# A windowed-attention layer and a per-image depthwise convolution: another order for the first rounds

## The chip, the core and the metric

The kernel runs on one core of one Trainium2 chip. Its metric is the device time of the whole launch in microseconds. A core has five engines with a queue of instructions each: PE (TensorE, the matrix unit), DVE (VectorE), ACT (ScalarE), POOL (GpSimd) and SP (SyncE, which here issues transfers only). They meet through semaphores.

## The reference, cut to what matters

The input is x, 16 images of 192 channels and 56 x 56 pixels, float32. The first layer is one shifted-window attention block, the second a depthwise convolution whose taps are computed from each image:

```
h   = window(roll(norm(x; g1, b1), -3))             # windows of 7x7 = 49 tokens
q,k,v = (h @ qkv_w + qkv_b)                         # 6 heads of 32
a   = softmax(q*scale @ k.T + bias[rel] + mask)     # mask: -inf in windows cut by the shift
x1  = x + unroll(a @ v @ proj_w + proj_b)
y   = x1 + gelu(norm(x1; g2, b2) @ fc1_w + fc1_b) @ fc2_w + fc2_b
t   = relu(batchnorm(mean(y) @ w1.T));  wt = t @ w2.T + b2    # taps of each image
out = depthwise3x3(y, wt * causal mask) + bias
```

All the products are in float32.

## The kernel before, in words

**Tiling.** The 192 channels are 3 groups (G) of 64; the 128 partitions hold 64 channels of two different window rows. An image has 8 window rows, so 4 steps of two window rows each (NU = 4); the launch has S = 64 steps. A step's tokens are 392 (UT) on each half.

**Rounds.** The loop `for r in range(-2, S + 3)` (L1620) is a software pipeline. In a steady round r it runs the scores and values of step r, the weighted sum, projection and residual of step r-1, the first feed-forward layer of step r-2 and the second of step r-3, the queries and keys of step r+1 and the first norm's statistics of step r+2. Rounds -2 to 2 are shorter: they have no feed-forward layers yet, but they load the parameters and fold the norms' gains and shifts into the weights.

**Who does what in a step.** `statistics` (L292) squares on ACT and adds the three groups on POOL into `fold`. In the early rounds `full_deviations` (L381) turns them, with a product against the constant block `full` (four recorded products, L387), into the reciprocal deviations `rb[:, 0]` on all partitions: PE, then ACT (L395), DVE (L402), ACT (L409, L413). Later rounds use `deviations` (L312), which computes a few rows only (L322) and spreads them through a buffer in memory, `rsd`, with three transfers on SP (L369, L378). `scaled1` (L424, mostly POOL, L436 and L447) multiplies x by `rb` into `xs`; `scaled2` (L459, POOL) does so for the second norm. `queries_keys` (L470) makes three products: part 0 is read by ACT into q (L491), part 1 by DVE into kbd (L502), and part 2 (heads 4 and 5) by ACT and DVE in turns into q2 and kbd2 (L515, L525, L534). `scores` (L544) makes three products j = 0, 1, 2 (L558) and for each a chain: add the bias table (DVE L584), maximum (DVE L595), subtract (POOL L600), exp (ACT L607), sum and reciprocal (DVE L612, L613), multiply (POOL L618). `values` (L653) makes three products (L673) that ACT copies (L689), and sends them in eight transfers on SP (L699). `turn_shares` (L622) turns the shares on DVE (L629) and sends them in ten transfers on SP (L635); `turn_values` (L704) turns the values (DVE L708). `weighted` (L711) makes the weighted sums (L728), copied out of PSUM by ACT (L755) and, for j = 1, by DVE (L757). `projection` (L773; L799, L785) is added to x by DVE (L827). `first_layer` (L831, L838) and `second_layer` (L856, L876) follow.

**PSUM.** Four tiles of two banks go round in the order in which the program takes them (`bank`, L187), so a product may wait for the reader of the tile four takings earlier.

**Parameters.** `load_qkv` (L1280) brings the attention weights raw, in five column blocks and two copies, ten transfers, half on SP and half on ACT. `small_loads` (L1203) puts eleven small vectors on ACT's queue; `small_columns` (L1236) transposes them on PE. `fold_qkv` (L1396) and `fold_fc1` (L1454) take the channel means off the weights: `centred_weights` (L1354) with wide products (L1362) and DVE (L1378), `shift_products` (L1333) with products of one column (L1342); `fold_qkv_rest` (L1415) and `fold_v` (L1427, L1435) do the rest for heads 4 and 5 and for the values. `biases_of_positions` (L1470) builds the bias tables `bt1` and `bt2` from transfers through memory (L1493, L1507), the masks (L1481) and twelve sums on DVE (L1522); half of them (r = 1) serve only an image's last step.

**The order.** Every operation is given to `Plan.add` (L53) with its engine, an assumed duration, what it reads and writes, and for transfers an assumed time to land (`lag`) or a fixed due time (`by`). `Plan.order` (L72) keeps PE's operations in the order of the program, derives due times for the others from that, and on each other engine always takes the operation that can start first, and among those the one due first. So PE's order is written by hand in the loop, and the others' follows from the assumed durations.

```
late[i] = ideal[i] if op[0] == "PE" else ideal[i] + op[5]
...
key=lambda j: (max(ready[j] - free[e], 0.0), late[j], j),
```

## Time and profile before

| | |
|---|---|
| three runs | 2743.76, 2746.55 and 2738.92 us, median 2743.76 us |
| the profiled execution | 2747.47 us, of which the span from first to last instruction is 2745.6 us |
| mean granted clock of PE | 0.995 |
| busy share | PE 98%, DVE 72%, ACT 62%, POOL 57% |
| PE from 0 to 150 us | 123.17 us busy, granted clock 0.92 |
| PE from 150 to 400 us | 249.83 us busy, granted clock 1.00 |
| PE from 2690 us to the end | 45.04 of 55.6 us busy |
| start of the first feed-forward product (L838) | 119.69 us |

In the views, "PE" is a product and "PEld" a load of weights for it; "SPq" and "ACTq" are transfers being issued. A row of the view by stretches gives the stretch and its length, the busy time and count of PE, PEld, DVE, ACT and POOL, the granted clock of PE, the busy share of the transfer engines and their rate. A row of the timeline gives start, length, engine, line and operation, the count, and in brackets the idle time before it with what ended it. The profile records one product of the program as two instructions; counts here are those of the records.

### The profile page before, as it was taken

The page shows a single profiled execution, that of the slowest core. Times are in us where ns is not written, and L with a number is a line of the kernel's source. Part 1 is how long each engine was busy: PE and PEld are TensorE (multiplying, and loading weights), DVE is VectorE, ACT ScalarE, POOL GpSimd, SP SyncE. Part 2 cuts the span into 40 slices and gives each one's busy share as a digit, 9 for nine tenths or more (in the row PEclk, how much of TensorE's full clock was granted, in tenths as well). Part 3 has the DMA queues.
Part 4 walks back from the last instruction along what each step waited for, and adds up shares of the span by engine and source line. Part 5 has one row for each costly group of instructions (what it writes and reads, how often), then busy time and mean ns, then how long its engine had stood idle before and what let it go on. Part 6 is the DMA issues. An engine that isn't in the chain of part 4 may idle for free.

```text
span 2745.6 us, 78133 instructions
## 1 busy us (share of the span) xinstructions
PE 2703.0 (98%) x32871; PEld 1669.1 (61%) x32871; DVE 1966.0 (72%) x3462; ACT 1714.7 (62%) x2787; POOL 1552.0 (57%) x1433
## 2 busy tenths in 40 slices
PE   6999999999999999999999999999999999999998
PEld 4656666666666566566566566566566566666654
DVE  6765776767687676876768777676876767767674
ACT  4556667657567566666666666576666666676553
POOL 6565565565565565565665555555655655655532
PEclk9899999999999999999999999999999999999999
DMA  5623343334425334343343424344253343433231
GB/s 124 127 51 72 83 111 71 86 83 104 92 67 117 69 86 101 72 116 72 78 104 90 106 67 96 73 103 92 67 129 69 75 110 80 113 72 73 60 77 52
DMA packets 142563, 239.61 MB, mean 87 GB/s; under 512 B 35148, under 2 KB 100612, under 8 KB 142212
## 3 DMA queue, kind: packets, MB, share of 16 engines
q1 hardware_dynamic: 140360, 232.95, 37.9%
q8 instruction: 258, 4.23, 0.7%
q10 hardware_dynamic: 1852, 1.66, 0.3%
q14 instruction: 93, 0.76, 0.1%
HBM read 66.81 MB, written 38.98 MB: 39 GB/s over the span
## 4 chain that ended last, share of the span: by engine, by line
PE 96%; DVE 2%; SPq 1%; DMA 0%; issue 0%; ACT 0%; POOL 0%; ACTq 0%; DVEq 0%
PE ps L876 28%; PE ps L838 28%; PE ps L478 14%; PE ps L673 7%; PE ps L558 5%; PE ps L799 5%; PE ps L728 5%; PE ps L785 2%; PE ps L322 2%; DVE sq L972 0%; PE ps L1362 0%; DVE hid L1152 0%; DMA tt<-in_L_conv_qkv_w_dram 0%; PE ps L1342 0%; DVE bt L1522 0%
## 5 line engine op out<-in xcount | busy, mean ns | idle before, releaser
L876 PE MATMUL ps<-hid,wf 128*64 128x392 f32 x4608 | 774.3, 494 | 0.5 <-issue 0.5
L838 PE MATMUL ps<-xs,wf 64*128 64x392 f32 x4608 | 769.5, 489 | 0.0
L838 PEld LDWEIGHTS ps<-xs,wf 64*128 64x128 f32 x4608 | 445.9, 187 | 312.6 <-issue 0.9
L876 PEld LDWEIGHTS ps<-hid,wf 128*64 128x64 f32 x4608 | 330.0, 137 | 408.2 <-issue 369.8
L306 POOL TENSOR_TENSOR fold<-sq 128x392 f32<-128x392 f32 x127 | 129.6, 1021 | 692.9 <-PE ps L322 684.3
L618 POOL TENSOR_TENSOR e<-e,tot 128x784 f32<-128x784 f32 x192 | 321.4, 1685 | 212.2 <-DVE tot L613 208.6
L850 ACT ACTIVATE hid<-ps,b1f 128x784 f32<-128x784 f32 x384 | 342.0, 913 | 137.3 <-PE ps L838 135.0
L478 PE MATMUL ps<-xs,wqkv 64*128 64x392 f32 x2304 | 402.6, 499 | 3.5 <-DVE x L827 1.5
L1152 DVE SCALAR_TENSOR_TENSOR y<-x,wt,y 128x770 f32<-128x770 f32 x270 | 319.1, 1201 | 66.2 <-ACT y L1014 45.3
L478 PEld LDWEIGHTS ps<-xs,wqkv 64*128 64x128 f32 x2304 | 218.6, 188 | 164.9 <-issue 17.0
L600 POOL TENSOR_TENSOR e<-e,top 128x784 f32<-128x784 f32 x192 | 283.3, 1504 | 41.6 <-DVE top L595 41.6
L491 ACT ACTIVATE q<-ps,qbs 128x400 f32<-128x400 f32 (+1 forms) x128 | 68.5, 589 | 319.6 <-PE ps L478 319.6
L612 DVE TENSOR_REDUCE tot<-e 128x16 f32<-128x784 f32 x192 | 182.2, 949 | 107.6 <-ACT e L607 107.6
L755 ACT COPY o<-ps 32x392 f32<-32x392 f32 x512 | 244.3, 477 | 9.5 <-PE ps L728 3.2
L629 DVE STREAM_TRANSPOSE tt<-e 128x512 f32<-128x512 f32 x384 | 245.7, 684 | 1.9 <-POOL e L618 0.4
L766 ACT ACTIVATE x<-x,vecs 128x392 f32<-128x392 f32 x192 | 105.7, 613 | 208.2 <-POOL xs L447 203.5
L343 DVE TENSOR_TENSOR m<-ps,m 128x196 f32<-128x196 f32 (+1 forms) x64 | 23.2, 363 | 273.5 <-ACT m L336 273.5
L673 PE MATMUL ps<-xs,wqkv 64*64 64x196 f32 x4608 | 204.7, 327 | 3.4 <-issue 1.4
L463 POOL TENSOR_TENSOR xs<-x,rb 128x392 f32<-128x392 f32 x192 | 193.5, 1039 | 25.0 <-DMA rb<-rsd 25.0
L306 POOL TENSOR_TENSOR fold<-x 128x392 f32<-128x392 f32 x128 | 132.8, 1038 | 127.7 <-DVE x L827 99.8
L436 POOL TENSOR_TENSOR xs<-x,rb 128x343 f32<-128x343 f32 x191 | 186.0, 1003 | 22.2 <-DMA rb<-rsd 16.8
L584 DVE TENSOR_TENSOR e<-ps,bt 128x784 f32<-128x784 f32 x192 | 175.3, 968 | 12.5 <-ACT hid L850 7.4
(134 smaller groups left out, 3688.1 us busy)
## 6 DMA issues: line engine op xcount, KB each, us to landing
pt<-tt SPq DMA_DIRECT2D x256, 192.0 KB
vb<-kbd SPq DMA_DIRECT2D x488, 96.0 KB
x<-in_x_dram SPq DMA_DIRECT2D x112, 294.0 KB
out_dram<-y SPq DMA_DIRECT2D x135, 196.0 KB
pt<-tt SPq DMA_DIRECT2D x256, 96.0 KB
rb<-rsd SPq DMA_DIRECT2D x118, 196.0 KB
out_dram<-y SPq DMA_DIRECT2D x45, 154.0 KB
x<-in_x_dram SPq DMA_DIRECT2D x16, 168.0 KB
```

Source lines behind the costliest of these rows:

```text
L306: at.tensor_tensor(f, src[:, 0], src[:, 1], ALU.add)
L463: nc.gpsimd.tensor_tensor(xs2[:, g], xv[:, g], rb[:, 1], ALU.mult)
L478: nc.tensor.matmul(p[:, ab, 0:UT], lhs_qk(ab, g, i), d[P(ab), g, 0:UT], start=(g == 0), stop=(g == G - 1), tile_position=(64 * ab, 0),)
L600: nc.gpsimd.tensor_tensor(ev, ev, top[j].broadcast_to([128, 16, N]), ALU.subtract)
L618: nc.gpsimd.tensor_tensor(ev, ev, tot[j].broadcast_to([128, 16, N]), ALU.mult)
L629: nc.vector.transpose(tt[:, kb, 16 * j : 16 * j + 16], src)
L673: nc.tensor.matmul(p[P(wh), ab, 0 : 4 * N], wqkv[P(ab), g, 2 * DIM + 64 * m : 2 * DIM + 64 * m + 64], xs[P(ab), g, wh * 4 * N : (wh + 1) * ...
L755: add("ACT", 0.5, lambda dst=dst, src=src: nc.scalar.copy(dst, src), [k], [("o", j, i)])
L838: nc.tensor.matmul(p[:, ab, 0:UT], wf1[P(ab), g, f * 128 : (f + 1) * 128], xs2[P(ab), g], start=(g == 0), stop=(g == G - 1), tile_position ...
L850: nc.scalar.activation(hid[:, f], p[:, :, 0:UT], AF.Gelu, bias=b1f[:, f : f + 1])
L876: nc.tensor.matmul(p[P(ab), 0, 0:UT], wf2[:, f, g * 64 : (g + 1) * 64], hid[:, f, ab], start=(f == 0), stop=(f == NFC - 1), tile_position= ...
L1152: nc.vector.scalar_tensor_tensor(dst, s_, w[:, g, t : t + 1], dst, ALU.mult, ALU.add)
```

## The change

- **Unread products.** A new helper `warm` issues n products with `full` as weights into the PSUM tile that is next in turn, which nobody reads: eleven of 128 columns at the very start, two of 392 after the first x has come, two after its square, two after the first `rb`, two after the first `xs`.
- **Weights in two transfers.** `load_qkv` brings the whole matrix once on SP and once on ACT. The columns then lie in the order of the input, so `centred_weights` writes four blocks with their own keys, and part 2 takes its columns from two places.
- **Transfers elsewhere.** The masks go to ACT's queue; the transfers of the bias rows get due times ahead of the load of step 1, which itself is due earlier.
- **Bias tables in two parts** with a key each, (bt, 0) and (bt, 1); only an image's last step reads the second. Their assumed duration is larger.
- **Another order of PE.** In round 0 what is still to fold, part 2 of the queries and `fold_v` move from round -1 to between the scores j = 1 and j = 2. In round 1 the first value product of step 1 stands before the scores j = 2. `weighted(0)` moves ahead of the value products of step 2. In round 2 `scaled1(3)` and the queries of step 3 come before `fold_fc1`, and the first norm of step 4 moves behind the projection.
- **fc1's fold.** Its wide products and its products of one column alternate instead of following each other.
- **Step 0's second norm** takes `full_deviations(1)` instead of `deviations([1])`, so without the transfers through memory. `deviations([1])` stays in round 3.
- **Copies.** For steps 0 and 1 the copies of j = 1 go from DVE to ACT. The assumed time to land of the shares is 2.5 instead of 7 us for steps 0 to 2.

The diff, cut to its core:

```
+    def warm(n, src, keys):
+        i = taken[0] % 4
+        def go():
+            for _ in range(n):
+                nc.tensor.matmul(ps[i][:, 0, 0 : src.shape[1]], full, src, start=True, stop=True)
+        add("PE", n * 0.00167 * src.shape[1], go, keys + ["blk"], [("ps", i, 0), ("ps", i, 1)])
...
-    def full_deviations():
+    def full_deviations(n=0):
...
-    def scores(s):
+    def scores(s, amid=None):
...
+            if j == 2 and amid is not None:
+                amid()
...
-            add("DVE", 0.98, biased, [pk, "bt"] + ["variance"] * (j == 0), [("e", j)])
+            add("DVE", 0.98, biased, [pk, ("bt", 0), ("bt", int(last))] + ["variance"] * (j == 0), [("e", j)])
...
-                lag=7.0,
+                lag=7.0 if s > 2 else 2.5,
...
-        yield
+            yield
...
-                if j != 1:
+                if j != 1 or s < 2:
...
+        dup(
+            lambda p: wraw[p],
+            wv,
+            [("wqkvl",)],
+            queues=("SP", "ACT"),
+            dur=0.8,
+            by=-99.5,
+            lag=7.0,
+        )
...
         def means():
-            for i, at, pieces_ in parts:
-                lo, hi = pieces_[0][0], pieces_[-1][1]
+            shifts = shift_steps(n, chunks, p)
+            for i, lo, hi, _ in parts:
                 for g in range(G):
                     nc.tensor.matmul(
...
+                    next(shifts, None)
...
-            add("SP", 0.72, go, [], [("relrows", yq)], lag=4.0, by=-79.0)
+            add("SP", 0.72, go, [], [("relrows", yq)], lag=3.5, by=-98.0)
...
-                    add("DVE", 0.2 + 0.1 * (hi - lo), go, keys, ["bt"])
+                    add("DVE", 0.1 + 0.32 * (hi - lo), go, keys, [("bt", r)])
...
+    def last_heads():
+        fold_qkv_rest()
+        queries_keys(0, (2,))
+        fold_v()
...
-            load(1, -80.0, 5.0)
+            load(1, -97.0, 5.0)
+            warm(11, full, [])
+            statistics(0, 0)
+            warm(2, rows(0)[:, 0].rearrange("p r c -> p (r c)"), X(0))
+            warm(2, sq[:, 0], ["sq"])
             small_columns(0)
-            statistics(0, 0)
...
+        if has(r) and r != 2:
+            ahead = values(r)
+            scores(r, {0: last_heads, 1: lambda: next(ahead)}.get(r))
+            for _ in ahead:
+                pass
+        if r == 2:
             scores(r)
+            scaled1(3)
+            queries_keys(3, (0, 1, 2))
             fold_fc1()
+            full_deviations(1)
+            scaled2(0)
+            weighted(1)
+        if r == 3:
             deviations([1])
...
+            if r == -1:
+                warm(2, rb[:, 0], RB(0))
             scaled1(r + 1)
-        if early and r > -2:
+        if -2 < r < 2:
             if r == -1:
+                warm(2, xs1[:, 0], [("xs1", 0)])
                 queries_keys(0, (0, 1))
-                fold_qkv_rest()
-                queries_keys(0, (2,))
-                fold_v()
...
+        if has(r - 1) and r != 2:
+            weighted(r - 1)
         if r == 1:
             ahead = values(2)
-            next(ahead)
+            for _ in range(G):
+                next(ahead)
             fold_taps()
-        if has(r - 1):
-            weighted(r - 1)
...
+        if r == 2:
+            full_deviations()
```

## The prediction

> **What bounds the kernel now.** First the page's parts 1 and 2: PE is the bound, and only the first slice shows room.
>
> ```profile
> span 2745.6 us, 78133 instructions
> ...
> PE 2703.0 (98%) x32871; PEld 1669.1 (61%) x32871; DVE 1966.0 (72%) x3462; ACT 1714.7 (62%) x2787; POOL 1552.0 (57%) x1433
> ```
>
> Next the view by stretches (PE's busy time is the third column; after POOL's comes the granted clock):
>
> ```profile
> 0.00:10.00 10.00, 0.00 (x0) 0.00 (x0) 4.16 (x15) 0.00 (x0) 9.15 (x18) 1.00 0.66 129
> 30.00:40.00 10.00, 4.85 (x117) 3.61 (x120) 9.14 (x15) 4.38 (x8) 4.45 (x4) 0.97 0.66 169
> 70.00:80.00 10.00, 7.03 (x118) 5.18 (x120) 7.64 (x14) 7.75 (x17) 7.12 (x6) 0.85 0.44 96
> 80.00:90.00 10.00, 9.72 (x175) 7.58 (x171) 7.73 (x19) 5.46 (x11) 3.67 (x6) 0.64 1.00 204
> 110.00:120.00 10.00, 7.81 (x146) 6.55 (x140) 8.01 (x15) 8.07 (x16) 6.51 (x7) 0.83 0.52 108
> ```
>
> PE idles 26.8 us in the first 150, and 4.9 between 150 and 2400. So the first rounds, up to L838 at 119.69, are all that the change can win. Of the 26.8, 10.75 pass before the first product; the waits of PE name the rest:
>
> ```profile
> PE ps L1244 <- DMA hid<-in_L_conv_proj_b_dram: 10.8, 1, 10.8
> PE ps L558 <- DVE bv L1448: 4.3, 1, 4.3
> PE ps L558 <- ACT q L515: 3.1, 2, 2.2
> PE ps L728 <- ACT y L689: 2.2, 1, 2.2
> PE ps L799 <- ACT o L755: 1.1, 1, 1.1
> ```
>
> The second loss is the clock. By stretches of 2 us:
>
> ```profile
> 38.00:40.00 2.00, 0.44 (x12) 0.44 (x16) 1.94 (x6) 0.00 (x0) 0.25 (x1) 0.87 0.00 0
> 42.00:44.00 2.00, 2.00 (x44) 1.62 (x40) 2.00 (x3) 0.90 (x4) 1.89 (x2) 0.78 0.00 0
> 76.00:78.00 2.00, 0.14 (x3) 0.01 (x1) 1.97 (x4) 1.97 (x5) 2.00 (x3) 0.76 0.12 22
> 86.00:88.00 2.00, 2.00 (x20) 1.34 (x20) 0.84 (x4) 0.49 (x1) 0.00 (x0) 0.68 1.02 248
> 94.00:96.00 2.00, 2.00 (x12) 2.00 (x11) 1.44 (x2) 0.74 (x1) 1.92 (x3) 0.52 0.64 146
> ```
>
> A mean of 0.87 is 0.5 for the last 0.52 us, so the clock fell at 39.48; likewise it rose at 42.88, fell at 77.04, rose at 87.28, fell at 94.08. PE's timeline prices it, and shows a slow start too, which the clock column misses (it says 1.00):
>
> ```profile
> 10.93 2.98 PE L387 MATMUL ps<-fold,hid 128*128 128x392 f32 x4
> 20.55 6.81 PE L478 MATMUL ps<-xs,wqkv 64*128 64x392 f32 x24
> 51.84 1.58 PE L387 MATMUL ps<-fold,hid 128*128 128x392 f32 x4
> 91.10 5.14 PE L1342 MATMUL ps<-vecs,wf 64*128 64x1 f32 x36 [0.16 <-DVE x L827]
> 96.11 5.28 PE L1362 MATMUL ps<-wf,gs 64*128 64x384 f32 x12
> 102.11 6.20 PE L478 MATMUL ps<-xs,wqkv 64*128 64x392 f32 x36
> ```
>
> L387 is 2.98 slow, 1.58 fast; a part of L478 3.4 slow, 2.07 fast. Up to L838 slow products cost about 20 us (7 at the start, 2 at 40, 4.6 at 78, 4.4 in fc1's fold, 2 at 114), idling 16.1.
>
> **A rule against the rows.** The Trainium skill (TensorE: Matmul & The Clock Gate, Part 1) says that a free-running window of 3.41 us sets the clock: one busy window frees it, an idle one halves it. The changes above lie on such a grid: 77.04 - 39.48 is 11.0 windows, 94.08 - 77.04 5.0. But by the rule the products from 10.93 on should be fast by 17.8; the pairs of L478 keep 0.65 us spacing until 25.8. And under "HAM oscillation" only gaps near 3.4 us cost clock, while the fall at 77.04 follows a longest gap of 0.8 in its window, half filled with small products. By the rule the holes that I leave below (3.2 us and 2.6 us) would cost no clock, and the sum would gain 22; by the rows they cost 4, and it gains 18. I take the rows: a half-empty window loses the clock, and only a full one brings it back.
>
> **The change, part by part**, as PE's own timeline, fast rates unless said.
>
> *A, to the end of the first two parts (27.36 before).* Eleven unread products are 22 records of 128 columns; at L387's slow rate (2.98 for 4 x 392) 5.3 us, from 1.7 to 7.0, while PE has nothing else. x lands at 6.69; the larger weight rows now share the engines with it, so I add 0.5 (bounds: 0, as the ACT half of the weights shared them before too; 1.0). Two unread pairs, 1.5 each if fast, end before the first sums at 11.2 (10.75 + 0.5). Were they still slow, 7.0 + 2 x 2.98 = 13, costing 1.8: the upper bound; I take 0. Then L387 to 12.8; L1362 4.21 halves to 2.2, 15.0; twelve one-column products at 0.1 (20 in 2.00 us at 92:94) 1.4; the transpose 0.3: 16.7. `rb` comes 2.35 after L387 (13.91 to 16.26 before): 15.15; POOL needs 1.93 + 0.98 for xs: 18.1, or 19.1 with a fold ahead. The two unread pairs, 1.5 each, end at 19.7, so they, not xs, set the start: price 0.6 to 1.6. L478 4.15: 23.9. Gain 3.5. The ten weight transfers made two take 4.2 us off the issuing queue of SP and 3.0 off ACT's; the seven L1493 (5.54) now stand ahead of step 1's x, whose sums PE first needs at 23.9 (before, they were done 7 us after x landed; x may land at 14). The four masks go behind the small vectors on ACT's queue, 4 x 0.36 = 1.4, ahead of the table load and L395; that queue ended at 11.55 before and now ends some 1.6 earlier even so. The wqkv blocks become twelve DVE instructions of 0.3 to 0.4 instead of nine, + 0.9 on an engine that idles from 22.6 to 27.4. No cost for these; if ACT's queue ran 1 us past L395, 1 us.
>
> *B, to the queries of step 1 (45.72 before, 18.4 long).* L387 1.5; wait for kbd (DVE 2.1 after the product) 0.7; scores j = 0, 1 1.5; the rest's fold 0.6; part 2 2.1; fold_v 1.2. Then scores j = 2 needs q2: ACT and DVE alternate, 4.3 us from 29.93 to 34.28 before. fold_v covers 1.2 of it, so PE now waits 3.2: this takes the place of the 4.3 behind the bias tables (L1522 held DVE 7.05 us). Of their 8.05 us the first half, 3.0, is due now, the second in round 3. The 3.2 us empty a window, so j = 2 and the values (0.75 + 3.0) run partly slow, + 2.2. Sum 17.0. Gain 1.4.
>
> *C, to the queries of step 2 (18.2 long).* 6.2 + 1.55 + 2.2 + 3.0 = 12.95. The value product of 1.0 put ahead of j = 2 covers part of the q2 wait (2.25 before): 0.8 left. XS(2): before, 10.5 us passed from L387's end at 53.42 to 63.95, 4.3 of them with L402 queued on a full DVE (9.2 and 9.6 of 10 from 50 to 70). With the bias tables out of the way I take 7.2 (least: 1.9 + 0.6 + 3.6 = 6.1); wait 1.2. Sum 15.0. Gain 3.2.
>
> *D, to the end of projection(0) (25.0 long).* 6.2 + 1.55 + weighted 2.2 + values 3.0 + 0.35 + projection 3.3 = 16.6. weighted(0) no longer stands behind ACT's copies of values(2) (2.2), and the values now cover its own copies: twelve on ACT at 0.49, 5.9 us, against 3.9 beside DVE's 2.3. I leave 1.9 of waits for them, no clock loss. Sum 18.5. Gain 6.5. The shares' ten transfers (7.0 us of SP) must land before weighted(0), near 63.6: j = 2 of step 0 ends 6 us earlier than before, and DVE, freed of the bias tables, should end the turning at some 52 to 55 instead of 62; 55 + 7 + 2 is 64. The shorter assumed time to land changes the order only; I cost it at nothing (0 to 2).
>
> *E, to L838 (30.8 long).* 2.2 + 6.2 + fold + 1.55 (`full_deviations(1)`, 0.75 over L322) + 2.2 + 3.3 + 1.55. The fold: 10.4 before; at fast rates 2.2 + 3.6 = 5.8, up to 8 if a window of it halves the clock. Nothing stands between weighted(1) and the projection, which waits for eight ACT copies, 3.9, less the 1.3 that overlaps: 2.6. Removing the way through memory (L322 at 101.3 to L463 at 117.7) costs nothing on PE's path any more: xs2 would be ready 4 us early, and the sums that `full_deviations(1)` reads are there 6 us ahead of it (projection(0) ends near 74; DVE 2.1, ACT 1.2 and POOL 4 follow). Its three SP transfers go. The first norm of step 4, moved behind the projection, is wanted in round 3, beyond the 12 us of L838. Clock and small waits 2.0 (0 to 5). Sum 27.4. Gain 3.4.
>
> Together 18.0 us; L838 near 101.7. After it PE was full before, and stays so: the tail is untouched.
>
> **Rivals.**
> 1. *Clock held, waits filled (22%).* Without B's 2.2, C's 2.0, half of D's 1.9 and E's 2.0: 7.2 more, 2718.5. For: the unread products stand where PE waits. Against: B's hole has none.
> 2. *DVE, ACT and SP become the bound (22%).* DVE has 81.2 us of work from 10 to 120; less 4.5 for the copies moved and 3.0 for the second bias half, 74 in the 90 that are left. If XS(2) keeps its 10.5 (+3.3), shares land late (+2) and ACT's twelve copies push keeps and projections (+3): gain 9.7, 2734.
> 3. *Slower: the clock stays halved (3%).* From B's hole on no window is full until projection(0): 33 us of fast work take twice as long, 27 net of waits: 9 lost, 2753. It decides where slow work exceeds 18 us. Against: the 6.2 us of queries, 12.4 slow, hold full windows.
> 4. *It does little (3%):* the slow start merely moves; gain 2 to 5.
>
> **How the numbers follow.** The forecast has 50%. The profiled execution took 2747.47, 1.9 over its span and 3.7 over the median 2743.76; minus 18.0 it gives 2729.5, the median 2725.8. The range 2714 to 2737 takes rival 1 with 4 us for the phase of the clock's windows, and most of rival 2. About 0.3%, 8.2 us, can be told from no change: faster 0.87 (the forecast, rival 1 and two thirds of rival 2), same 0.10 (the rest of rival 2 and rival 4), slower 0.03.
>
> **What would show it.** L838 near 102; the first L478 at half its 6.81; a hole of 3 us before scores j = 2 of step 0, with a fall of the clock; L1342 and L1362 alternating in 5 to 6 us; L402 soon after L395. Wrong if L838 starts after 112, or if the waits of PE name SP's L635 or POOL's xs for more than 5 us.

## The result: 0.27% faster, two fifths of the gain forecast

The changed kernel takes 2738.17 us, the median of 15 runs (2736.35 to 2742.71); 15 runs of the kernel before gave 2746.44 (2738.92 to 2751.55). The ratio is 0.9973, with a 95% interval of 0.9965 to 0.9981: 7.4 us of 2746. The interval leaves 1 out, so a gain is there; it is smaller than the 0.3% that the prediction named as what can be told from no change. The time is 12 us above the predicted 2725.8 and 1.2 above the range of 2714 to 2737. The profiled execution took 2740.57, 2.1 over its span.

Line numbers move: below L851 is the forecast's L838, L889 its L876, L571 its L558, L489 its L478, L398 its L387, L741 its L728, L812 its L799, L686 its L673, L620 its L607, L1345 and L1378 its L1342 and L1362. The unread products are L200. In the experiments' kernels some of these lines are one lower or higher (L1377, L1344, L1479), and where `values` grew, L741 is L778 and L812 is L849.

First the page's parts 1 and 2 of the kernel after.

```profile
span 2738.5 us, 78187 instructions
...
PE 2707.5 (99%) x32911; PEld 1667.4 (61%) x32911; DVE 1959.8 (72%) x3457; ACT 1717.2 (63%) x2795; POOL 1555.3 (57%) x1433
```

PE is busier than before and yet the time is nearly the same: of the 40 records more, 38 are unread ones. Busy time says nothing here. The view by stretches, in three of the windows shown of before:

```profile
0.00:10.00 10.00, 6.00 (x25) 5.25 (x26) 2.37 (x14) 0.00 (x0) 7.40 (x17) 0.95 0.72 150
30.00:40.00 10.00, 7.28 (x119) 5.48 (x120) 8.98 (x16) 6.02 (x11) 8.08 (x9) 0.83 0.84 185
70.00:80.00 10.00, 7.64 (x127) 5.56 (x129) 6.84 (x14) 9.80 (x23) 1.99 (x2) 0.86 0.88 191
```

The stretch 70 to 80 is the one to look at: PE has 2.4 us idle and a clock of 0.86, ACT is busy for 9.80 us (7.75 before) and POOL for 1.99 (7.12 before). The waits of PE up to 120 us:

```profile
PE ps L571 <- ACT q L526: 2.7, 2, 2.3
PE ps L200 <- DMA x<-in_x_dram: 2.2, 1, 2.2
...
PE ps L812 <- ACT o L768: 1.7, 2, 1.4
PE ps L686 <- ACT q L526: 1.4, 1, 1.4
PE ps L571 <- DVE kbd L513: 1.1, 1, 1.1
PE ps L686 <- DVE e L597: 1.1, 1, 1.1
PE ps L741 <- ACT q L526: 0.9, 1, 0.9
PE ps L812 <- ACT y L702: 0.8, 1, 0.8
```

The waits of 10.8 and 4.3 of before are gone. Those of 0.2 to 2.3 have not become fewer: without the two large ones the waits of before add up to 11.9 us, and those of after to 17.0. PE's timeline, at the places that the forecast priced:

```profile
8.55 2.49 PE L200 MATMUL ps<-x,hid 128*128 128x392 f32 x4 [2.24 <-DMA x<-in_x_dram]
10.83 2.29 PE L200 MATMUL ps<-sq,hid 128*128 128x392 f32 x4
...
13.21 1.58 PE L398 MATMUL ps<-fold,hid 128*128 128x392 f32 x4
...
21.60 4.22 PE L489 MATMUL ps<-xs,wqkv 64*128 64x392 f32 x24
...
77.11 3.89 PE L812 MATMUL ps<-o,wp 128*64 128x196 f32 x24 [0.75 <-ACT y L702]
...
99.27 2.98 PE L398 MATMUL ps<-fold,hid 128*128 128x392 f32 x4
102.18 3.44 PE L741 MATMUL ps<-pt,v 49*64 49x100 f32 x96
...
107.82 3.88 PE L812 MATMUL ps<-o,wp 128*64 128x196 f32 x22 [1.42 <-ACT o L768]
...
114.30 12.12 PE L851 MATMUL ps<-xs,wf 64*128 64x392 f32 x72
```

The slow start is cured (L489 4.22 instead of 6.81), but the clock is lost again and again later: L812 takes 3.9 twice where 2.2 is the fast length, L398 2.98 instead of 1.58. L851 starts at 114.30, against 119.69 before and 101.7 in the forecast. This start of the first feed-forward product is called the landmark below. By the forecast's segments:

| PE, us | before | forecast | after |
|---|---|---|---|
| A, to the end of the first two parts | 27.36 | 23.9 | 25.75 |
| B, to the queries of step 1 | 18.4 | 17.0 | 16.3 |
| C, to the queries of step 2 | 18.2 | 15.0 | 17.0 |
| D, to the end of projection(0) | 25.0 | 18.5 | 23.1 |
| E, to the first feed-forward product | 30.8 | 27.4 | 32.2 |
| gain at that product | | 18.0 | 5.4 |

From there to the end 2624.2 us pass, 2625.9 before: what is won by then is kept. The difference of 1.7 says nothing, as in the ten profiles below of kernels that change little or nothing behind the landmark this rest is 2622.3 to 2628.2 us long.

### The profile page after: what moved, and what is told of

The parts are those of the page before. It is cut to its first block, busy times and chain, and to the rows that moved or that the text cites. A ratio compares the mean times of both kernels' runs of the same rounds, so it can differ in the third digit from the quotient of the medians.

```text
span 2738.5 us, 78187 instructions
## 1 busy us (share of the span) xinstructions
PE 2707.5 (99%) x32911; PEld 1667.4 (61%) x32911; DVE 1959.8 (72%) x3457; ACT 1717.2 (63%) x2795; POOL 1555.3 (57%) x1433
## 3 DMA queue, kind: packets, MB, share of 16 engines
q10 hardware_dynamic: 1152, 1.74, 0.3%
## 4 chain that ended last, share of the span: by engine, by line
PE 96%; DVE 2%; DMA 1%; ACT 1%; SPq 0%; issue 0%; POOL 0%; ACTq 0%; DVEq 0%
PE ps L889 28%; PE ps L851 28%; PE ps L489 14%; PE ps L686 7%; PE ps L571 5%; PE ps L741 5%; PE ps L812 5%; PE ps L798 2%; PE ps L333 2%; DVE sq L985 0%; DMA x<-in_x_dram 0%; DVE x L840 0%; DVE hid L1165 0%; DVE trow L984 0%; ACT o L768 0%
## 5 line engine op out<-in xcount | busy, mean ns | idle before, releaser
L889 PE MATMUL ps<-hid,wf 128*64 128x392 f32 x4608 | 774.2, 494 | 0.4 <-issue 0.4
L851 PE MATMUL ps<-xs,wf 64*128 64x392 f32 x4608 | 769.5, 489 | 0.0
L851 PEld LDWEIGHTS ps<-xs,wf 64*128 64x128 f32 x4608 | 445.9, 187 | 312.9 <-POOL xs L474 1.2
L889 PEld LDWEIGHTS ps<-hid,wf 128*64 128x64 f32 x4608 | 327.8, 137 | 410.4 <-issue 379.3
L489 PE MATMUL ps<-xs,wqkv 64*128 64x392 f32 x2304 | 400.3, 496 | 3.2 <-DVE x L840 2.5
L1165 DVE SCALAR_TENSOR_TENSOR y<-x,wt,y 128x770 f32<-128x770 f32 x270 | 312.7, 1177 | 66.1 <-ACT y L1027 45.2
L489 PEld LDWEIGHTS ps<-xs,wqkv 64*128 64x128 f32 x2304 | 216.4, 187 | 164.8 <-issue 13.0
L686 PE MATMUL ps<-xs,wqkv 64*64 64x196 f32 x4608 | 205.2, 327 | 3.3 <-ACT q L526 1.4
```

The lines of the kernel that those rows point to most:

```text
L489: nc.tensor.matmul(p[:, ab, 0:UT], lhs_qk(ab, g, i), d[P(ab), g, 0:UT], start=(g == 0), stop=(g == G - 1), tile_position=(64 * ab, 0),)
L686: nc.tensor.matmul(p[P(wh), ab, 0 : 4 * N], wqkv[P(ab), g, 2 * DIM + 64 * m : 2 * DIM + 64 * m + 64], xs[P(ab), g, wh * 4 * N : (wh + 1) * ...
L851: nc.tensor.matmul(p[:, ab, 0:UT], wf1[P(ab), g, f * 128 : (f + 1) * 128], xs2[P(ab), g], start=(g == 0), stop=(g == G - 1), tile_position ...
L889: nc.tensor.matmul(p[P(ab), 0, 0:UT], wf2[:, f, g * 64 : (g + 1) * 64], hid[:, f, ab], start=(f == 0), stop=(f == NFC - 1), tile_position= ...
L1165: nc.vector.scalar_tensor_tensor(dst, s_, w[:, g, t : t + 1], dst, ALU.mult, ALU.add)
```

## The experiments

All have a ratio to the kernel before, taken beside it; as that one took 2745.6 to 2749.4 us beside the different kernels, ratios are compared and not times. Theory: PE isn't the bound of the first rounds; at some places it meets a chain of ACT, DVE and SP that is no earlier than before, and PE's gains end in waits there. Rivals: the lost clock alone is what is missing; one named part of the change costs what another gains; or the engines beside PE are full as a whole and no order helps. The last column of this table is worked out: the shift of the landmark against after (L851; for the three kernels marked *, which move the first feed-forward layer, the second layer's start against 134.54), over 2746, added to 0.9973.

| kernel | ratio (95%) | landmark, us | from the landmark |
|---|---|---|---|
| after | 0.9973 (0.9965 to 0.9981) | 114.30 | |
| e1, both weight halves behind x | 0.9971 (0.9959 to 0.9984) | 111.97 | 0.9965 |
| e2, copies back on DVE | 0.9963 (0.9951 to 0.9976) | 110.94 | 0.9961 |
| e3, fold not alternating | 0.9970 (0.9959 to 0.9981) | 112.42 | 0.9966 |
| e4, second norm by memory | 0.9988 (0.9981 to 0.9995) | 113.80 | 0.9971 |
| e5, no unread products | 0.9978 (0.9968 to 0.9988) | 116.24 | 0.9980 |
| e6, e1 and bias rows late | 0.9960 (0.9947 to 0.9974) | 111.86 | 0.9964 |
| e7, fold in the holes | 0.9983 (0.9976 to 0.9989) | 117.25 | 0.9984 |
| e8, layer ahead of projection * | 0.9954 (0.9941 to 0.9966) | 130.15 | 0.9957 |
| e9, landing time 7.0 | 0.9982 (0.9974 to 0.9990) | 114.06 | 0.9972 |
| e10, e7 and e9 | 0.9973 (0.9963 to 0.9983) | 113.93 | 0.9972 |
| e11, e1, e2, e7, e8, e9 * | 0.9972 (0.9961 to 0.9983) | 132.63 | 0.9966 |
| e12, e1, e2, e8 * | 0.9974 (0.9963 to 0.9986) | 131.07 | 0.9960 |
| e13, without e4's, e5's, e9's part | 0.9988 (0.9979 to 0.9996) | 117.44 | 0.9984 |

One landmark of one profile gives the ratio to within 0.0007 in ten of the thirteen; e9 lies 0.0010 above it, e12 0.0014, e4 0.0017. From before's landmark after's own ratio would be 0.9980, 0.0007 off. The intervals are 0.0007 to 0.0014 wide to each side, so most of these kernels can't be told from after by their ratio: only e8 lies below it and e4 and e13 above it with intervals that barely meet. What the experiments show, they show in their timelines. In e4's profile the span from L851 on is 2628.1, 3.9 longer than in after; 1.5 of that is one gap of PE between 160 and 400 that no awaited engine explains, the rest has no place that the profile names. e7 has 2628.2 there and fits its landmark.

**e1**, the first term of A that failed: x landed at 8.5, because ACT's half of the weights shares the engines with it.

```
-            queues=("SP", "ACT"),
```

> The changed kernel, with both transfers of the attention weights on SP's queue behind the first x, so that none on ACT's queue shares the transfer engines with x. Theory 1 (x came 1.8 us later than before, at 8.5, because the ACT half of the weights, now one transfer of 432 KB, shared the engines; the empty stretch behind the eleven unread products then lost the clock): x lands at 6.2 to 6.9, the clock doesn't fall near 9, L398 of step 0 starts at 11.0 to 11.3 instead of 13.2, and the whole is 1.5 to 2 us faster than the changed kernel, about 2736. Theory 2 (the first rounds are bound by the sum of DVE, ACT and SP work, and a gain at the start is given back in the waits behind it): L398 starts earlier, but L851 stays within 0.7 us of 114.3.

x lands at 6.05, the first unread pair follows at once, the clock isn't lost there. PE's timeline of e1:

```profile
9.77 1.58 PE L398 MATMUL ps<-fold,hid 128*128 128x392 f32 x4
...
28.65 1.59 PE L571 MATMUL ps<-kbd,q 64*64 64x98 f32 x64 [2.98 <-DVE kbd L513]
```

L398 comes 3.4 us earlier than in after, the scores j = 0 no earlier (28.41 in after). The 3.4 us end in front of it, in the waits for DVE (1.68 at step 1's L398, 2.98 for kbd). DVE's timeline of e1 shows why:

```profile
22.92 0.94 DVE L1571 TENSOR_TENSOR bt<-hid 128x294 f32<-128x294 f32 x1 [4.99 <-DMA x<-in_x_dram]
23.79 0.14 DVE L1450 TENSOR_TENSOR bq<-ps,qkvb 128x2 f32<-128x2 f32 x1
...
24.89 1.61 DVE L1571 TENSOR_TENSOR bt<-hid 128x294 f32<-128x294 f32 x2
26.42 2.08 DVE L513 TENSOR_SCALAR kbd<-ps,bq,mask 128x784 f32<-128x784 f32 x2
```

DVE sits idle for 4.99 us in front of a bias sum whose rows come through memory, and the query bias and kbd are queued behind it. (The row names a load of x; in after the same sum waits for `hid<-relrows`, the transfer that it reads.) The planner had taken the rows to be there sooner.

e1 also settles what the lost clock is worth. The stretch up to the landmark, in after and in e1:

```profile
0.00:114.30 114.30, 97.28 (x1123) 66.48 (x1123) 83.43 (x156) 61.71 (x118) 70.66 (x77) 0.90 0.65 138
0.00:111.97 111.97, 89.71 (x1123) 61.15 (x1123) 82.62 (x156) 61.55 (x118) 70.48 (x77) 0.97 0.66 141
```

The same 1123 records take 7.6 us less in e1, since the clock is kept at 9, 77 and 94. Of that, 5.2 us come back as waits (PE idles 22.3 instead of 17.0), 2.91 of them for step 1's shares, and the landmark is 2.3 us earlier. So the lost clock alone is not what holds the first rounds: give it back, and PE waits for the other engines. The ratio, 0.9971, can't show the 2.3 us that are left.

**e6** gives the planner longer times for them: `lag` 3.5 to 6.0 for L1543 and 2.5 to 9.0 for L1557, on top of e1.

> The changed kernel with both weight transfers on SP behind x, and in addition larger assumed times to land for the bias rows (6 and 9 us instead of 3.5 and 2.5), which puts the sums of the bias tables behind kbd in DVE's order. Theory 2 (DVE stood in front of the bias sums until 22.9, waiting for their rows by way of memory, and q's bias and kbd were queued behind): kbd comes at 23 to 25 instead of 28.5, scores j = 0 starts at 24.5 to 26, and the whole is 1 to 3 us faster than with x first alone. Rival (the chain of DVE as a whole is full): scores j = 0 starts earlier, but the queries of step 1 start within 0.7 us of 42.7.

The scores j = 0 come at 25.64, 3.0 us earlier than in e1, and PE then waits where the bias sums now stand. PE's timeline of e6:

```profile
33.79 2.08 PE L1479 MATMUL ps<-vecs,tt 64*64 64x1 f32 x36 [4.11 <-DVE e L597]
```

4.11 us; the queries of step 1 start at 41.78, 0.94 earlier than in e1 (42.72) and 0.24 earlier than in after. That is a little outside the 0.7 that the rival of full engines allowed, but most of the 3.0 us is gone, and at L851 (111.86) 0.1 is left. In after DVE has 8.98 of 10 us of work from 30 to 40 and 9.27 from 50 to 60, which speaks for that rival here. The ratio, 0.9960 against e1's 0.9971, can't tell the two apart.

**e2** gives a third of the copies of steps 0 and 1 back to DVE (`if j != 1:`).

> The changed kernel, with the copies of j = 1 of steps 0 and 1 on DVE again, as before the change. Theory 1 (ACT's twelve copies, 5.9 us in a row, are what PE waits for in front of both projections: 2.2 us at step 0 and 1.7 at step 1, and they empty windows of the clock): the waits of L812, L1628 and L686 on ACT shrink by 1.5 to 2.5 us in all, and the whole is 1.5 to 3 us faster than the changed kernel. Theory 2 (DVE is the fuller engine there, 9 of 10 us): DVE's chains come later by the 4.5 us that it takes back, and the whole is the same or up to 2 us slower.

The waits for copies among the value products go, and one of 2.39 for ACT's y, one of 1.21 for DVE's x and one of 1.14 for DVE's o come. L851 starts 3.4 us earlier than in after; the ratio, 0.9963, is not apart from after's.

**e3** issues the fold's one-column products first and the wide ones then.

> The changed kernel, with fc1's fold as before the change: the 36 records of one column first, then the 12 wide ones, not alternating. Theory 1 (alternating gains nothing: a step of one wide product and six records of one column took 1.31 us at either clock, 8.35 us in all[...], and the clock fell at 94.4 all the same): apart, at the fast clock 3.6 + 2.2 = 5.8 us, with a fall of the clock inside up to 8.5; the whole is within 1.5 us of the changed kernel. Theory 2 (the forecast's: alternating saves the clock, and apart costs the 10.4 us of before): 2 us slower or more.

The two take 5.59 and 4.71 us, 10.1 in all against 8.35 in after: more than the first theory had, as much as before the change. Yet L398 (1.58) and L812 (2.20) behind them are fast, and L851 comes 1.9 us earlier than in after: the second theory's 2 us are not lost. How long the alternating fold takes depends on the clock: where it was kept, it took 5.9 to 6.0 us (e1, e8, e12, e13), the forecast's figure.

**e4** takes step 0's second norm back to memory (`deviations([1])` in round 2).

> The changed kernel, with step 0's second norm by way of memory again (deviations([1]) in round 2). The forecast said that the way through memory costs nothing on PE's path: then the product is 0.75 to 2.1 us shorter (L333 for L398) and the whole is 0 to 1.5 us faster. The other theory: from the small product to xs2 it took 16.4 us before (101.3 to 117.7), and L851 now would follow after 15.0 (99.3 to 114.3), so it waits for xs2: L851 starts 1 to 4 us later than its products allow, and the whole is 1 to 3 us slower.

PE's timeline of e4 seems to have the way through memory in front of the weighted sum:

```profile
100.94 4.66 PE L741 MATMUL ps<-pt,v 49*64 49x100 f32 x96 [2.80 <-DMA rsd<-rs]
```

The name misleads: the weighted sum reads the shares (`pt`) and the values (`v`), not `rsd`. SP has issued the shares by 95.4 here and by 95.6 in e1, where PE waits until 100.39 and the row names `pt<-tt`; so this is the wait for the shares again. Where the way through memory could hold PE up, in front of L851, e4 has no wait: L398 runs from 112.29, L851 from 113.80. From the queries of step 3 (83.29; 84.44 in after) to L851 e4 takes 30.5 us, after 29.9. In this profile the part costs nothing on PE's path, as the forecast had it. The ratio says more, 0.0015, with intervals that touch, and by the landmark it should have been no slower. So the part is worth 0 to 4 us, and no trace shows where.

**e5** leaves out the unread products (`warm` returns at once).

> The changed kernel without any unread product. Theory 1 (they keep the clock in A): the first products up to about 25 run at half speed as before the change, the queries of step 0 end at 28 to 29 instead of 25.8, and the whole is 2 to 4 us slower than the changed kernel. Theory 2 (the run of the weights with x first has shown that scores j = 0 of step 0 starts at 28.4 to 28.7 however early PE is ready, because kbd comes then): A's slow products are covered by that wait, and the whole is within 1.5 us of the changed kernel.

L489's first parts take 7.25 instead of 4.22 and the scores j = 0 come at 31.93 instead of 28.41: 3.5 us are lost at 30. At L851 1.9 are left. The cure of the slow start is real, and nearly half of it is given back on the way. The 0.0005 in the ratio (1.4 us) is within both intervals.

**e7** puts the fold's one-column products into the holes behind the value products of steps 1 and 2, and the last six behind the transposes of the taps.

```
+                for f in extra.get(m, ()):
+                    fc1_shift(p, 0, f)
...
-            chunks,
...
+            ahead = values(r, {0: (0, 1)} if r == 1 else {})
...
+            ahead = values(2, {0: (2,), 1: (3,), 2: (4,)})
```

> The changed kernel with fc1's products of one column taken out of the fold and put, six records each, behind value products of steps 1 and 2 and into the transposes of the taps, where PE waits. Theory 1 (the alternating fold costs 8.35 us and the clock behind it): the fold takes 2.2 us, step 0's second norm and weighted(1) run at full speed, and the whole is 4 to 6 us faster than the changed kernel. Theory 2 (the shares of step 1, turned by DVE at 89.8 and issued by SP until 95.8, then bound weighted(1), which with a fast clock already waited 2.9 us for them in the run with x first): weighted(1) starts at 98 to 100 and the whole is 0 to 2.5 us faster.

The fold takes 2.95, the L398 behind it comes at 96.83 and is fast. Then PE's timeline of e7 has the largest wait behind A of all these kernels:

```profile
96.83 1.58 PE L398 MATMUL ps<-fold,hid 128*128 128x392 f32 x4
104.47 4.66 PE L778 MATMUL ps<-pt,v 49*64 49x100 f32 x96 [6.05 <-DMA pt<-tt]
```

Step 1's shares are not there before 104. In after the fold hides that. (The products in the holes cost something themselves: the queries of step 2 start 4.4 us later than in after.) Take the fold away, and the wait and a lost clock (4.66 instead of 2.5) stand in its place. The first theory's 4 to 6 us are not there; the second had foreseen the wait, though not its length.

**e8** fills that place with work that is ready: the norm of step 4 and the first feed-forward layer go between the weighted sum and the projection of step 1, step 1's second norm moves behind the weighted sum of step 2 in round 3.

> The changed kernel with another order of round 2: the first norm of step 4 and the first feed-forward layer of step 0 come between weighted(1) and projection(1), and step 1's second norm in round 3 moves behind weighted(2). Theory 1 (projection(1) waits 1.65 us for ACT's copies, and the emptied window makes it run slow, 2 us): both go, and the whole is 2 to 4 us faster than the changed kernel. Theory 2 (a new wait takes their place, since xs2 needs 5 to 6 us from the second norm's product and ACT now has copies and feed-forward activations at once): 0 to 1.5 us faster, or slower.

Ratio 0.9954, the best of the study; its interval and that of after just touch (0.9966, 0.9965). The wait for the copies (1.65) and the slow L812 are gone, since 12 us of products stand ahead of it:

```profile
106.10 12.49 PE L851 MATMUL ps<-xs,wf 64*128 64x392 f32 x72 [0.34 <-ACT o L768]
118.52 2.21 PE L812 MATMUL ps<-o,wp 128*64 128x196 f32 x24
```

The weighted sum of step 1 still starts at 101.73, much as in after (102.18), e1 (100.39), e2 (100.78) and e6 (100.11). Why are its shares late? ACT's timeline of after:

```profile
70.06 5.87 ACT L768 COPY o<-ps 32x392 f32<-32x392 f32 x12
75.95 2.00 ACT L702 ACTIVATE y<-ps,bv 128x256 f32<-128x256 f32 x6
77.80 0.65 ACT L420 ACTIVATE rb<-rb,eps 128x392 f32<-128x392 f32 x1
78.31 0.89 ACT L620 ACTIVATE e<-e 128x784 f32<-128x784 f32 x1
...
79.48 0.88 ACT L620 ACTIVATE e<-e 128x784 f32<-128x784 f32 x1
```

The last two exponentials of step 1 and the roots of step 3's first norm stand behind twelve copies and six keeps. The change's shorter assumed landing made them look less urgent.

**e9** undoes that line alone (`lag=7.0`), **e10** does so in e7.

> One part of the change undone: the planner is told again that a turned share takes 7.0 us to land in steps 0 to 2 (the change says 2.5). Nothing else is touched. On ScalarE this puts step 1's last two exponentials (L620) and the roots of step 2's norm in front of the 12 copies L768 and the 6 keeps L702, where they stood before the change. Theory (gains on TensorE are given back because ScalarE and VectorE hand step 1's shares on late): the two exponentials begin by 74 instead of at 78.31 and 79.48, VectorE turns step 1's last share by 85 instead of 88.5, and it lands by 91 instead of at about 96; the copies come some 2.8 us later and projection(0) with them (end 84 to 85 instead of 82.1). As the fold and L398 keep TensorE busy until 102 in the changed kernel, the time alone moves by less than 2: 2736.5 to 2740, ratio 0.9965 to 0.9978. Rival (the engines are full as a whole, the order is worth nothing): the share lands after 94 even so, and the time is 2738 to 2741. If the lag of 2.5 was itself worth something, 2741 to 2744.

> e7_fold_in_holes with the assumed landing of 7.0 us from e9. In e7, with the one-column products of the fold gone from their place, TensorE waited 6.05 us for step 1's last share (its weighted values began at 104.47 and ran slow after it) and the kernel was no faster than before (2745.1). Theory (the late exponentials of step 1 make that wait): the wait falls to under 2.5 us, the weighted values begin at 97 to 101, the window behind L398 is no longer half empty, so the clock is held over them, and the time is 2737 to 2740, 5 or more below e7. Rival (VectorE's turning and SyncE's transfers set it whatever ScalarE does first): the wait stays at 4 or more, and the time at 2743 to 2746.

The order acts as argued (the roots are those of step 3's norm; step 2 in the expectation is a slip). ACT's timeline of e9:

```profile
72.29 0.84 ACT L620 ACTIVATE e<-e 128x784 f32<-128x784 f32 x1
...
73.45 0.84 ACT L620 ACTIVATE e<-e 128x784 f32<-128x784 f32 x1
74.20 5.86 ACT L768 COPY o<-ps 32x392 f32<-32x392 f32 x12
```

DVE's last turn of the shares ends at 80.7 instead of 89.8. But the copies come 4.1 us later, and PE's timeline of e9 pays for it among step 2's values:

```profile
76.18 1.57 PE L686 MATMUL ps<-xs,wqkv 64*64 64x196 f32 x24 [2.48 <-ACT o L768]
```

Projection(0) ends at 84.6 (82.1 in after), L851 starts at 114.06, and the time, 2741.15, missed both the theory's range and the rival's; it lies in the third, 2741 to 2744, which stood for the 2.5 being worth something by itself (ratio 0.9982; its interval and that of after overlap). In e10 the wait of 6.05 on the shares is gone altogether. The time, 2738.81, lies in the theory's range, but the kernel before ran 4 us faster beside e10 than beside e7; by the ratios (0.9983 and 0.9973) e10 gains 0.0010, 2.7 us, where 5 or more were expected, and the intervals overlap. The weighted sum starts at 103.58, where 97 to 101 was expected. The view by stretches of e10 shows what took its place:

```profile
76.00:78.00 2.00, 0.24 (x3) 0.16 (x2) 1.97 (x4) 1.97 (x5) 0.62 (x2) 1.00 1.07 219
78.00:80.00 2.00, 1.90 (x30) 1.56 (x30) 1.97 (x4) 1.94 (x5) 2.00 (x2) 0.94 1.15 219
80.00:82.00 2.00, 2.00 (x26) 1.49 (x25) 2.00 (x5) 1.93 (x5) 1.48 (x2) 0.50 1.06 221
...
88.00:90.00 2.00, 2.00 (x18) 1.16 (x18) 0.00 (x0) 0.00 (x0) 0.00 (x0) 0.50 1.01 135
```

PE waits at 76 for the late copies, the clock falls at about 79.8 and stays at half for 10 us, through all of projection(0) (L849, 4.19 instead of 2.2).

**e11** and **e12** put together what had moved a landmark alone.

> Everything together that moved a step by itself: both halves of the weights behind x on SyncE's queue (e1), a third of the copies on VectorE (e2), the fold's one-column products in the value products of steps 1 and 2 (e7), the full norm of step 4 and the first feed-forward layer in front of step 1's projection (e8), the assumed landing of 7.0 us (e9). Theory: each hole that took back one part's gain is filled by another, so the parts add here where they did not alone: weighted values of step 1 at 96 to 99, first feed-forward product by 102, time 2730 to 2734 (ratio about 0.994). Rival (VectorE, ScalarE and SyncE are full from 28 to 100, whatever the order): weighted values at 100 or later, first feed-forward product at 104 to 106 as in e8, time 2735 to 2738.

> e8_layer_first (2736.4) with the weights' halves both behind x (e1) and a third of the copies on VectorE (e2); the fold stays where the change puts it. Theory: as the fold fills TensorE until step 1's shares are there, the two additions move the start of the fold by 2 to 3 us and the weighted values by 1 to 2, so 2734 to 2736. Rival (full engines): 2736 to 2738, no better than e8, with the wait on the shares longer by what TensorE comes earlier.

Both missed: 0.9972 and 0.9974, no better than after. In e11 the clock is at half from 76 to 89.6; in e12 PE waits 2.30 for DVE's x (e2, with the same copies on DVE, waits 1.21 there, after not at all), and the queries behind it run slow (7.89 instead of 6.20). The parts don't add. e12 has one thing to show, its fold at full clock, in PE's timeline:

```profile
95.30 0.89 PE L1377 MATMUL ps<-wf,gs 64*128 64x384 f32 x2
96.03 0.72 PE L1344 MATMUL ps<-vecs,wf 64*128 64x1 f32 x6
...
98.91 0.51 PE L1377 MATMUL ps<-wf,gs 64*128 64x384 f32 x1
98.93 0.47 PE L1344 MATMUL ps<-vecs,wf 64*128 64x1 f32 x3
```

From 94.07 to 100.00 it takes 5.9 us; in after the clock fell in it at 94.36, and it took 8.35.

**e13, e14 and e15** ask what the order of the rounds is worth by itself. e13 takes the three parts away together whose ratios alone were the worse ones (e4, e5, e9); e14 and e15 put one of them alone into the kernel before: step 0's second norm without memory, and the landing time of 2.5.

> The changed kernel with three of its parts undone at once: no unread products (e5), step 0's second norm through memory again (e4), the assumed landing of 7.0 us (e9). What stays of the change is the order of the first rounds, the weights in two transfers, the bias tables in two parts, ScalarE's copies and the fold with its two kinds of products in turn. Undone one at a time the three lost 0.0005, 0.0015 and 0.0009 of the ratio. Theory A (they carry the whole of the measured gain and add up; the parts that stay are worth nothing to the time): ratio 0.9995 to 1.001, 2744 to 2748. Theory B (the order of the rounds and the halves carry the gain, and each of the three is partly given back by the others): ratio 0.997 to 0.9985, 2738 to 2741. In between: the parts overlap.

> The kernel before with one part of the change alone: step 0's second norm computed for all 128 partitions at once, without the way through memory; 8 products L322 on 32-wide blocks give way to 2 pairs of full ones, one root chain on ScalarE over 392 columns takes the place of the copies to memory and back. If e4's 4 us belong to this part by itself (it takes a transfer out of the chain in front of the first feed-forward layer): first feed-forward product at 116 to 118 instead of 119.69, ratio 0.998 to 0.9992, 2741 to 2744. If they came only of the place that the change gives it (weighted values behind it, TensorE idle meanwhile): ratio 0.9995 to 1.0005, as in the kernel before TensorE has the q/k products and weighted values of 11 us between the statistics at 101.32 and the first feed-forward product.

> The kernel before with one line of the change alone: the assumed landing of a turned share is 2.5 us in steps 0 to 2. On ScalarE this moves only the roots of step 2's norm behind the copies of step 0's weighted values, and little on the other engines. If the lag is worth what e9 showed (0.0009) by itself: ratio 0.9985 to 0.9995, 2741 to 2744. If it acts only through the order that the change gives the rounds: ratio 0.9995 to 1.0005.

e13: 0.9988, between the two theories. The three together are worth about 0.0015, the sum of their single losses is 0.0029; that they overlap is likely and not shown, as each of these figures is uncertain by about 0.001. What stays of the change is worth 0.0012 (0.0004 to 0.0021), some 3 us; no run splits this further. In e13 PE does wait for the way through memory, 1.48 us in front of L851, and 3.48 in front of the weighted sum for DVE, which reads the fold. e14: 1.0002 (0.9993 to 1.0011). e15: 1.0004 (0.9995 to 1.0013). In the old order neither part is worth anything that can be measured, and the least gains that were named for the other case, 0.0008 and 0.0005, lie just outside the interval and at its edge. PE's timeline of e14 shows it for the norm:

```profile
98.98 1.58 PE L387 MATMUL ps<-fold,hid 128*128 128x392 f32 x4
...
111.55 0.92 PE L728 MATMUL ps<-pt,v 49*64 49x100 f32 x32 [1.81 <-ACT q L515]
113.51 4.19 PE L799 MATMUL ps<-o,wp 128*64 128x196 f32 x24 [1.05 <-ACT o L755]
...
119.61 12.12 PE L838 MATMUL ps<-xs,wf 64*128 64x392 f32 x72
```

PE is 2.3 us early in this profile at 99, and the first feed-forward product starts at 119.61, where it did before (119.69). In e15's profile it starts at 122.52.

## Why the prediction was wrong, by its own steps

The step that failed is the forecast's picture of the first rounds as PE's own products at fast rates plus a few priced waits. PE's next meetings with ACT, DVE and SP were put too low (XS(2) 7.2 us, ACT's copies 1.9) or at nothing (step 1's shares in front of weighted(1), kbd when PE comes early), and so was the clock that the waits cost (nothing in A and D). In its place the runs show a chain of other engines that PE runs into: of 18.0 us forecast at the landmark 5.4 came, and where e1 gave PE 7.6 us of clock back, 5.2 turned into waits. By its steps:

- **What bounds the kernel: right in place, wrong in kind.** The landmark carries the time in most kernels. But e1, e6 and e7 show that PE has slack ahead of it: 3.4, 3.0 and 3.9 us won at one place (L398 13.21 to 9.77; scores j = 0 28.65 to 25.64; fold and L398 over at 98.4 instead of 102.3) end in a wait further on.
- **A, 1.9 short.** Two terms. x landed 1.8 later than before, beyond the bound of 1.0. And the unread pairs were slow (2.49 and 2.29): between the first eleven, which end at 6.3, and x PE had nothing to do for 2.2 us; the view by stretches has a clock of 0.76 from 8 to 10 and of 0.89 from 12 to 14, so it fell at 9.0 and was back at 12.4. That was the forecast's upper bound, costed at nothing. From L398 on all of A ran at the rates forecast (2.2, 1.4, 4.2).
- **B, right** (16.3 for 17.0; the terms given add up to 16.75): the hole at q2 took 2.7 us (3.2 forecast) and halved the clock, as the rows of before had said; the rule of gaps near 3.4 us (the Trainium skill, TensorE: Matmul & The Clock Gate, "HAM oscillation") would have let it pass. What was missed is that the scores in B can't start earlier than kbd allows.
- **C, 2.0 short: one term,** XS(2). 9.3 us passed from L398's end at 49.73 to 59.04, where 7.2 was taken "with the bias tables out of the way". DVE was still 9.27 of 10 busy from 50 to 60. Rival 2 had said so.
- **D, 4.6 short.** Waits of 3.7 for 1.9, and L812 slow (3.89 for 2.2) where no clock loss was costed: the window of 3.41 us before 77.3 held 1.8 us of products. Weighted sums and values took 1.2 more than priced. ACT's twelve copies in a row stand behind these waits, and e9 shows the other side of it: put the exponentials first, and PE waits for the later copies instead.
- **E, 4.8 short.** The fold, 8.35 for 5.8; its own upper case of 8, with the clock lost in it, came true. L398, L741 and L812 slow cost 4.2 more, where 2.0 stood for clock and small waits together. But e1, with a fast fold (6.04), L398 and L741, has a wait of 2.91 for step 1's shares in their place: the forecast had no such wait. In e1, e4, e6, e7 and e8 the shares, not the fold, set the start of the weighted sum, at 100.1 to 104.5. Removing the way through memory, costed at nothing, shows no cost on PE's path in e4 and none in the old order (e14); the ratio of e4 leaves room for up to 4.
- **The landing time,** "the order only; 0 to 2", does change the order, and by e9 it may be worth 2 us in the new order (0.0009, the intervals overlap) and nothing in the old one (e15). It is a trade between copies and exponentials.
- **The rivals.** Rival 2 (DVE, ACT and SP become the bound; 2734, gain 9.7) was nearest, in its mechanism and its sum; it had 22%. Its sum is near in part by luck, as it has no term for A or for more lost clock in D and E. "Wrong if L838 starts after 112" was the right test, and it was met.

The rule of the Trainium skill (TensorE: Matmul & The Clock Gate, Part 1) on windows of 3.41 us holds in after as a grid: the clock's means are 0.58 from 36 to 38, 0.82 from 76 to 78 and 0.59 from 94 to 96, so it fell at 36.32, 77.28 and 94.36, 12.0 and 5.0 windows apart. Which windows lose the clock is another matter. In after those ending at 9.0, 36.3, 77.3 and 108.0 held products for 31 to 53% of their length; the one from 50.0 to 53.4 with 58% kept it, so four waits of 0.35 to 1.4 in C cost only themselves. But the share of time is no rule, and neither is the forecast's "a half-empty window loses the clock, and only a full one brings it back". In before itself a window with 1.76 us of products kept it (32.65 to 36.06) and one with 1.74 lost it (73.61 to 77.02). In e1 one with 1.45 kept it (24.22 to 27.63, mostly L398), in e13 one with 2.42 lost it (33.58 to 36.99, half of that one-column products). The window before 94.36 was full of fold products and lost it, and in e10 PE is full from 80 to 90 with the clock at half all the way. The kind of the products may be what counts; no run varied it alone.

Three things stay open. Where e4 loses what its landmark doesn't show. What makes the fold lose the clock: it did in after, e2, e4, e5, e6 and e9 and not in e1, e8, e12 and e13. Where a window begins 0.0 to 2.0 us behind the fold's start (after, e2, e4, e6, e9), its end has the fall; where one begins 0.3 to 0.9 us ahead, four keep the clock and one, e5, does not. So the phase of the windows is the likely reason, and no run set it. And whether an order exists that feeds ACT's copies and exponentials both in time: each kernel here moved the late one.

## What to carry to other kernels

In a pipeline's filling rounds, price a gain of the busiest engine by the next place where it meets another engine's chain, and ask of that chain what makes it earlier; if nothing does, the gain is worth its way to that place and no more. When a part moves work from a full engine to another, look at what is queued behind it there (twelve copies in front of two exponentials), and when a planner's assumed durations are changed, read the new order on every engine, since it decides more than the edit shows. An edit's worth belongs to the order around it: in the old order two parts of this change moved nothing (1.0002, 1.0004), and in the new one three parts undone together cost about half the sum of their single losses, as far as such small differences can be told. And when a fast clock is what a gain counts on, ask first what PE would wait for if it had it: in e1 two thirds of the time that the clock gave back went into waits.

## What the runs showed of the hardware

- At full clock the alternating fold runs at two rates: in its first half two wide and six one-column products take 1.31 us (95.30 to 96.61 in e12), in its second half 0.67 (98.58 to 99.25). The first half's wide products read the same half of the rows as the one-column ones, the second half's the other. That the two then run side by side is what the overlapping records suggest; no run tried it alone. At half clock the second half takes 1.28 (after).
- A busy PE isn't enough to keep the clock: in after the fold's first half filled the window from 90.95 to 94.36 without a gap, and the clock fell at its end. Nor is it enough to bring it back: in e11 PE is busy without a gap from 76 to 88 at half clock.
- A small transfer can hold up a queue. The waits of SP in after:

```profile
SPq L1543 <- DMA hid<-in_L_conv_norm_b_dram: 6.7, 1, 6.7
```

The vector of 1.5 KB that ends this wait is issued at 2.69 on ACT's queue, behind 432 KB of weights, and SP goes on at 9.54. In e1, with no weights on that queue, SP's wait for such a vector is 2.3 us. That the place in the queue is the reason, and not only the load on the transfer engines, is not shown apart.
